# Two graph layers on one core: two batches' stages issued in turn instead of one batch after another

## The chip, the cores and the metric

The kernel runs on one core of one Trainium2 chip. The metric is the device time of one execution in microseconds; it is given as the median of several runs, and one further execution was taken with the hardware profiler. Work on the core is split over TensorE (PE; its weight loads are listed as PEld), VectorE (DVE), ScalarE (ACT), GpSimd (POOL), and the queue of SyncE (SP), which here issues transfers only. Each engine takes its instructions in the order in which the compiled program lists them.

## What is computed

There are 16 independent batches, each with 1024 nodes of 256 features (`x`, float32) and a 1024 x 1024 matrix of 0 and 1 (`adj`, int32). A batch goes through two layers.

```python
# layer 0: graph attention, 4 heads of 64
h = einsum('bnd,hde->bhne', x, W)
weight = leaky_relu(e_src[:, None] + e_dst[None, :]) where adj == 1, else -1e9   # e_* = h . a_*
out = relu(softmax(weight) @ h + bias) + h          # then a layernorm per head
x = layernorm(x + out)
# layer 1: self-attention, 8 heads of 32, queries = keys = values, then an MLP
y = layernorm(x) * gamma1 + beta1
o = x + softmax(mask(adj > 0, y y^T / sqrt(32))) @ y
o = o + (gelu(layernorm(o) @ W1 + b1) @ W2 + b2)    # 256 -> 1024 -> 256
x = layernorm(x + o)
```

The only work that crosses batches is the loading of constants. Both layers of one batch need the same mask.

## The kernel before

The program is one long list, unrolled over the 16 batches. A batch has four stages, and the next batch begins where the last stage ends.

**Preparation** (`prepare`, `masks`). The batch's `x` is loaded whole into `xb` (1 MB, by SP), turned on PE in four pieces (`transpose_rows`, L208, copied out by ACT, L209) and multiplied with the weights (`es`, L234; `h`, L243, copied out by DVE, L244). `cb` (L251, L253) holds the exponentials of the source terms for all heads and columns. `masks` takes eight row blocks of `adj`, which POOL's queue loads and casts to bf16 (L224), turns each on PE (L279), has DVE copy it from PSUM to the bf16 tile `mask` (L280), and has ACT square it for a range test (L281), after which the block's buffer is loaded again.

**Layer 0** (`attention0`, `after0`). For two column halves `n` and two head pairs, eight key blocks are gone through two at a time: four DVE instructions (L300, 128 x 512 each) make the unnormalised weights `p`, and 12 matmuls (L311, L321, column tiles of 32; float32, so each is two PE instructions) add up the products and the sums of the weights. After a half, `after0` runs for two pairs of row blocks: a chain of some 20 DVE instructions that goes over to POOL six times (L359, L373, L392 and the power function of L183) and to ACT once (L367), and that leaves `x1`, `v1` and, turned, `nT`.

**Layer 1** (`attention1`, `finish1`). There are 32 steps (two halves, two groups of four heads, eight key blocks). A step is four score matmuls (L407, row tiles of 32), ACT exponentials into two tiles `p` (L413, 128 x 1024), two DVE multiplications with the mask (L414), and, two steps later (`LAG = 2`), four product and four sum matmuls (L421, L429). `finish1` normalises a half, again over POOL (L485 to L487, L183), and its pieces are issued between later steps.

**MLP** (`mlp`). Per half, eight hidden tiles (L515, L518 with Gelu) and four output blocks (L525), each followed by a layernorm `z` on DVE and POOL (L529, L193, L188, L183, L201) and a store by SP (L531).

A tile pool has a number of buffers for each name of tile, and an instruction that writes a new tile waits until the last reader of the buffer's former tile is done. Eight PSUM banks are dealt out as `ps_s` (two tiles of two banks), `ps_t` (two of one) and `ps_o` (two of one). `mask`, `x1`, `v1`, `nT`, `xb`, and the tiles named `big` (`cb` and the MLP's hidden tile) and `fT` (`xT` and `yT`) have one buffer each, so most of the next batch can't begin before this one has let go of them. The tile `p` has seven.

The order of the program is not quite the order on the engines. What is written earlier goes first, but in the compiled list an instruction whose buffer or input was not expected to be free is passed by a later one. The trace shows it: four of the mask transposes (L279) run between the two groups of L251, which the program writes wholly before them.

Of the kernel before, what the change touches and what calls it, by code (L numbers as in the profile page):

```python
# [31 lines left out]
F32 = mybir.dt.float32  # L32
# [18 lines left out]
def fast_path(  # L51
# [47 lines left out]
    three = ctx.enter_context(tc.tile_pool(name="three", bufs=3))  # L99
    seven = ctx.enter_context(tc.tile_pool(name="seven", bufs=7))  # L100
    small = ctx.enter_context(tc.tile_pool(name="small", bufs=4))
    ps_s = ctx.enter_context(tc.tile_pool(name="ps_s", bufs=2, space=PSUM))
    ps_t = ctx.enter_context(tc.tile_pool(name="ps_t", bufs=2, space=PSUM))
# [33 lines left out]
    for src, dst in ((a_src, wsrc.rearrange("p c (h q) -> p c h q", q=Q)[:, :, :, 0]), (a_dst, w0e[:, :, D : D + H0])):  # L137
        a = one.tile([P, H0, HO, T], F32, name="big")
# [4 lines left out]
        for c in range(DC):  # L143
            t = two.tile([P, H0, HO], F32, name="nrm")
# [58 lines left out]
    def transpose_rows(dst, src, k):  # L203

        pt = ps_t.tile([P, DC, GB, P], F32, name="pt")
        for g in range(GB):
            for c in range(DC):
                nc.tensor.transpose(pt[:, c, g, :], src[:, g, c * P : (c + 1) * P], ident)  # L208
        nc.scalar.copy(dst[:, :, k * P : (k + GB) * P], pt.rearrange("p c g q -> p c (g q)"))  # L209


    xbs = {}

    def load_x(b):
        xbs[b] = one.tile([P, NB, D], F32, name="xb")
        nc.sync.dma_start(xbs[b], x[b].rearrange("(k p) d -> p k d", p=P))
# [3 lines left out]
    def load_adj(i):  # L220
        b, k = divmod(i, NB)
        if b < B:
            ak = adj_blocks[i] = three.tile([P, N], BF16, name="ak")
            nc.gpsimd.dma_start(ak, adj[b, k * P : (k + 1) * P, :])  # L224

    def prepare(xb, factors):

        xT = one.tile([P, DC, N], F32, name="fT")
        for k in range(0, NB, GB):
            transpose_rows(xT, xb[:, k : k + GB, :], k)  # L230
        es = ps_s.tile([P, NH, HALF], F32, name="ps")
        for n in range(NH):
            for c in range(DC):
                nc.tensor.matmul(  # L234
                    es[:, n, :], wsrc[:, c, :], xT[:, c, n * HALF : (n + 1) * HALF], start=c == 0, stop=c == DC - 1
                )
        esr = one.tile([P, NH, HALF], F32, name="x1")
        nc.scalar.copy(esr, es)
        h = one.tile([P, NB, D + H0], F32, name="h")
        for k in range(NB):  # L240
            ph = ps_o.tile([P, D + H0], F32, name="po")
            for c in range(DC):
                nc.tensor.matmul(ph, xT[:, c, k * P : (k + 1) * P], w0e[:, c, :], start=c == 0, stop=c == DC - 1)  # L243
            nc.vector.tensor_copy(h[:, k, :], ph)  # L244
# [769 lines left out]
```

## Time and profile before

| | |
|---|---|
| median of 3 runs | 5069.28 us (5067.32 to 5074.34) |
| profiled execution, its own time | 5062.94 us |
| span from first to last instruction | 5061.2 us |
| granted PE clock, mean over the span | 0.895 |
| busy: PE, DVE, ACT, POOL | 4257.7, 3072.4, 1632.3, 1145.1 us |
| first dense transposes of batch 0; batch 2; batch 3 | at 32.8; 656.6; 968.4 us |

The profile's page gives busy time by engine, the span in 40 slices (digits are tenths), the chain of waits followed back from the last instruction, and groups of instructions with busy time, count, mean duration and the idle time of the engine just before them, with what ended it. The trace can also be asked for stretches of time, for waits, and for single instructions in order.

### The profile page before, as it was taken

The page shows a single profiled execution, that of the slowest core. Times are in us where ns is not written, and L with a number is a line of the kernel's source. Part 1 is how long each engine was busy: PE and PEld are TensorE (multiplying, and loading weights), DVE is VectorE, ACT ScalarE, POOL GpSimd, SP SyncE. Part 2 cuts the span into 40 slices and gives each one's busy share as a digit, 9 for nine tenths or more (in the row PEclk, how much of TensorE's full clock was granted, in tenths as well). Part 3 has the DMA queues.
Part 4 walks back from the last instruction along what each step waited for, and adds up shares of the span by engine and source line. Part 5 has one row for each costly group of instructions (what it writes and reads, how often), then busy time and mean ns, then how long its engine had stood idle before and what let it go on. Part 6 is the DMA issues. An engine that isn't in the chain of part 4 may idle for free.

```text
span 5061.2 us, 60881 instructions
## 1 busy us (share of the span) xinstructions
PE 4257.7 (84%) x25121; PEld 1780.8 (35%) x25121; DVE 3072.4 (61%) x5213; ACT 1632.3 (32%) x2000; POOL 1145.1 (23%) x1160
## 2 busy tenths in 40 slices
PE   6797987979889798897978979789797897978978
PEld 3252342523325233252432524325243252422524
DVE  5647656466664656646566465664656656566565
ACT  1331424314143241432424223242232423324233
POOL 2222122221222212122121221212212122221221
PEclk9898998989889898898988989889798998988979
DMA  2000010100101001010010100101001010010000
GB/s 67 9 18 16 4 23 9 26 9 5 22 9 26 9 5 21 9 26 9 6 20 9 26 9 8 18 9 26 9 7 19 9 26 9 9 17 9 19 1 10
DMA packets 58992, 75.57 MB, mean 15 GB/s; under 512 B 7249, under 2 KB 41809, under 8 KB 58705
## 3 DMA queue, kind: packets, MB, share of 16 engines
q0 software_dynamic: 18432, 33.56, 4.3%
q1 hardware_dynamic: 35072, 33.56, 2.0%
q10 hardware_dynamic: 5200, 4.46, 0.3%
q8 instruction: 199, 3.26, 0.3%
q14 instruction: 89, 0.72, 0.0%
HBM read 88.35 MB, written 16.78 MB: 21 GB/s over the span
## 4 chain that ended last, share of the span: by engine, by line
PE 46%; DVE 24%; POOL 18%; issue 7%; ACT 2%; DMA 1%; POOLq 0%; DVEq 0%; ACTq 0%
PE ps L515 9%; PE ps L407 8%; PE po L421 7%; PE po L525 7%; PE po L429 7%; DVE p L300 6%; DVE p L414 6%; POOL r L183 5%; PE ps L311 3%; PE pt L208 2%; POOL o L373 2%; POOL v L392 2%; POOL o L485 2%; ACT p L413 2%; POOL o L359 1%
## 5 line engine op out<-in xcount | busy, mean ns | idle before, releaser
L414 DVE TENSOR_TENSOR p<-p,mask 128x1024 f32<-128x1024 f32 x1024 | 1231.5, 1235 | 403.2 <-ACT p L413 403.1
L413 ACT ACTIVATE p<-ps 128x1024 f32<-128x1024 f32 x1024 | 994.6, 1021 | 847.7 <-PE ps L407 843.9
L311 PE MATMUL ps<-p,v 128*32 128x512 f32 x4096 | 831.6, 628 | 126.3 <-DVE p L300 126.3
L407 PE MATMUL ps<-nT 32*128 32x512 f32 x4096 | 763.9, 714 | 71.2 <-ACT p L413 71.2
L300 DVE SCALAR_TENSOR_TENSOR p<-big,dinv,mask 128x512 f32<-128x512 f32 x1024 | 733.1, 757 | 1.8
L421 PE MATMUL po<-p,v 128*32 128x512 f32 x4096 | 645.8, 664 | 56.4 <-DVE p L414 56.0
L429 PE MATMUL po<-p,unit 128*32 128x512 f32 x4096 | 637.8, 642 | 0.0
L485 POOL TENSOR_TENSOR o<-o,x 128x512 f32<-128x512 f32 x64 | 110.7, 1729 | 1665.9 <-DVE o L480 1665.9
L321 PE MATMUL ps<-p,ranges 128*32 128x512 f32 x2048 | 472.8, 604 | 0.0
L407 PEld LDWEIGHTS ps<-nT 32*128 32x128 f32 x4096 | 246.2, 205 | 598.3 <-ACT p L413 443.9
L525 PE MATMUL po<-w_sb,big 128*128 128x256 f32 x2048 | 454.2, 380 | 0.0
L515 PE MATMUL ps<-fT,w_sb 128*128 128x512 f32 x1024 | 451.6, 594 | 0.0
L525 PEld LDWEIGHTS po<-w_sb,big 128*128 128x128 f32 x2048 | 385.4, 190 | 59.3 <-issue 7.7
L183 POOL TENSOR_TENSOR r<-v,mhalf 128x2 f32<-128x2 f32 (+1 forms) x320 | 218.1, 681 | 749.3 <-DVE v L188 749.3
L311 PEld LDWEIGHTS ps<-p,v 128*32 128x32 f32 x4096 | 190.7, 112 | 538.8 <-DVE p L300 359.3
L208 PE MATMUL pt<-ident,v 128*128 128x128 f32 x256 | 67.1, 413 | 299.6 <-POOL v L392 299.6
L518 ACT ACTIVATE big<-ps,b_sb 128x512 f32<-128x512 f32 x256 | 175.9, 687 | 386.1 <-PE ps L515 386.1
L515 PEld LDWEIGHTS ps<-fT,w_sb 128*128 128x128 f32 x1024 | 190.8, 190 | 228.5 <-issue 227.4
L429 PEld LDWEIGHTS po<-p,unit 128*32 128x32 f32 x4096 | 149.5, 118 | 342.1 <-issue 341.2
L529 DVE TENSOR_TENSOR z<-po,x 128x256 f32<-128x256 f32 x128 | 54.0, 422 | 354.6 <-PE po L525 354.4
L421 PEld LDWEIGHTS po<-p,v 128*32 128x32 f32 x4096 | 95.3, 112 | 444.5 <-DVE p L414 236.3
L209 ACT COPY nT<-pt 128x512 f32<-128x512 f32 x64 | 37.5, 586 | 635.6 <-PE pt L208 635.6
(105 smaller groups left out, 3726.6 us busy)
## 6 DMA issues: line engine op xcount, KB each, us to landing
ak<-in_adj_dram POOLq DMA_DIRECT2D x128, 256.0 KB, 3.7
xb<-in_x_dram SPq DMA_DIRECT2D x16, 1024.0 KB, 5.2
out_dram<-z SPq DMA_DIRECT2D x128, 128.0 KB, 1.7
w_sb<-in_L_gnn_W_dram ACTq DMA_DIRECT2D x2, 1024.0 KB, 8.3
big<-in_L_gnn_a_src_dram ACTq DMA_DIRECT2D x1, 640.0 KB, 6.3
big<-in_L_gnn_a_dst_dram ACTq DMA_DIRECT2D x1, 640.0 KB, 5.2
w0e<-in_L_gnn_W_dram ACTq DMA_DIRECT2D x8, 32.0 KB, 7.6
bias_r<-in_L_gnn_bias_dram ACTq DMA_DIRECT2D x1, 128.0 KB, 6.4
```

The costliest lines, as they stand in the source:

```text
L183: nc.gpsimd.tensor_tensor(r, src, mhalf[:, :n], op=OP.pow)
L300: nc.vector.scalar_tensor_tensor(p[:, e, :], cb[:, hd, cols], dinv[:, jb, hd : hd + 1], mask[:, jb, cols], op0=OP.max, op1=OP.mult,)
L311: nc.tensor.matmul(acc[at : at + Q, 0, :], v0[:, jb, pair * PAIR + e, q * Q : (q + 1) * Q], ps[jb][:, e, :], start=jb == 0, stop=jb == NB - 1,
L321: nc.tensor.matmul(acc[at : at + Q, 1, :], factors[:, jb, pair * PAIR + e : pair * PAIR + e + 1].to_broadcast([P, Q]), ps[jb][:, e, :], st ...
L407: nc.tensor.matmul(tiles[e // PAIR][:, e % PAIR, :], nT[q, quad, keys], nT[q, quad, cols], start=True, stop=True)
L413: nc.scalar.activation(p, t, AF.Exp, scale=SCALE1)
L414: nc.vector.tensor_mul(p, p, mask[:, jb, None, cols].to_broadcast([P, PAIR, HALF]))
L421: nc.tensor.matmul(av[e * Q : (e + 1) * Q, :], v1[:, jb, hd * HD : (hd + 1) * HD], ps[e // PAIR][:, e % PAIR, :], start=jb == 0, stop=jb = ...
L429: nc.tensor.matmul(sums[e * Q : (e + 1) * Q, :], unit[:, quad, :], ps[e // PAIR][:, e % PAIR, :], start=quad == 0 and jb == 0, stop=quad = ...
L485: nc.gpsimd.tensor_add(o, o, x1[:, blocks, :])
L515: nc.tensor.matmul(ph, w1_sb[:, c, f * P : (f + 1) * P], yT[:, c, cols], start=c == 0, stop=c == DC - 1)
L525: nc.tensor.matmul(po, hid[:, f, q * P : (q + 1) * P], w2_sb[:, f, :], start=f == 0, stop=f == FC - 1)
```

## The change

Two generators now issue the program. `layer0()` does preparation, masks and layer 0 of all batches in turn; `layer1()` does layer 1 and the MLP of all batches. Each yields a number at its cutting points, in units close to microseconds of PE work, and a loop at the end takes a piece from one or the other so that `layer0()` stays 1.15 batches ahead by these numbers. A yield of 0.0 changes neither count, so the loop goes on with the same stream there.

`mask` (now bytes), `dinv`, `x1`, `v1` and `nT` get two buffers. `x` is loaded in pieces of two row blocks (`xk`, two buffers), once for preparation and once again for `after0`; `xT` exists for two row blocks only; `cb` is made for one half and one pair at a time; `adj` blocks have two buffers instead of three; `oT` and `sT` one instead of two, and `y` is written over `o`; `p` has six buffers instead of seven, for both streams. In PSUM, `ps_s` becomes four tiles of one bank that scores, exponents, hidden tiles and all transposes share; layer 0's products and sums have two banks of their own (`ps_a`), and `ps_o` stays. A step's scores are four tiles, so ACT's exponential is four instructions of 128 x 512 instead of two of 128 x 1024.

The core of the diff:

```diff
-    three = ctx.enter_context(tc.tile_pool(name="three", bufs=3))
-    seven = ctx.enter_context(tc.tile_pool(name="seven", bufs=7))
+    six = ctx.enter_context(tc.tile_pool(name="six", bufs=6))
     small = ctx.enter_context(tc.tile_pool(name="small", bufs=4))
-    ps_s = ctx.enter_context(tc.tile_pool(name="ps_s", bufs=2, space=PSUM))
-    ps_t = ctx.enter_context(tc.tile_pool(name="ps_t", bufs=2, space=PSUM))
+    ps_s = ctx.enter_context(tc.tile_pool(name="ps_s", bufs=4, space=PSUM))
+    ps_a = ctx.enter_context(tc.tile_pool(name="ps_a", bufs=2, space=PSUM))
     ps_o = ctx.enter_context(tc.tile_pool(name="ps_o", bufs=2, space=PSUM))
...
-    def transpose_rows(dst, src, k):
-
-        pt = ps_t.tile([P, DC, GB, P], F32, name="pt")
+    def transpose_rows(dst, src):
+
+        pt = ps_s.tile([P, DC, GB, P], F32, name="ps")
         for g in range(GB):
             for c in range(DC):
                 nc.tensor.transpose(pt[:, c, g, :], src[:, g, c * P : (c + 1) * P], ident)
-        nc.scalar.copy(dst[:, :, k * P : (k + GB) * P], pt.rearrange("p c g q -> p c (g q)"))
-
-
-    xbs = {}
-
-    def load_x(b):
-        xbs[b] = one.tile([P, NB, D], F32, name="xb")
-        nc.sync.dma_start(xbs[b], x[b].rearrange("(k p) d -> p k d", p=P))
+        nc.scalar.copy(dst, pt.rearrange("p c g q -> p c (g q)"))
+
+
+    def load_x(b, k):
+        t = two.tile([P, GB, D], F32, name="xk")
+        nc.sync.dma_start(t, x[b, k * P : (k + GB) * P, :].rearrange("(g p) d -> p g d", p=P))
+        return t
...
-            ak = adj_blocks[i] = three.tile([P, N], BF16, name="ak")
+            ak = adj_blocks[i] = two.tile([P, N], BF16, name="ak")
...
+    def prepare(b, h, esr):
+
+            xk = load_x(b, k)
+            xT = two.tile([P, DC, GB * P], F32, name="xT")
+            transpose_rows(xT, xk)
+            yield 1.0
+            es = ps_s.tile([P, GB * P], F32, name="ps")
+                nc.tensor.matmul(es, wsrc[:, c, :], xT[:, c, :], start=c == 0, stop=c == DC - 1)
+            nc.scalar.copy(esr[:, k * P : (k + GB) * P], es)
+            for g in range(GB):
+                ph = ps_s.tile([P, D + H0], F32, name="ps")
+                for c in range(DC):
+                    nc.tensor.matmul(ph, xT[:, c, g * P : (g + 1) * P], w0e[:, c, :], start=c == 0, stop=c == DC - 1)
+                nc.vector.tensor_copy(h[:, k + g, :], ph)
+            yield 2.7
...
+    def masks(b, mask):
+            i = b * NB + k
+            ak = adj_blocks.pop(i)
+            pt = ps_s.tile([P, NB, P], BF16, name="ps")
+            for j in range(NB):
+                nc.tensor.transpose(pt[:, j, :], ak[:, j * P : (j + 1) * P], identb)
+            nc.vector.tensor_copy(mask[:, :, k * P : (k + 1) * P], pt)
+            nc.scalar.activation(ak, ak, AF.Square, bias=mhalf[:, 0:1], accum_out=types[:, i : i + 1])
+            load_adj(i + 2)
+            yield 1.0
...
+    def attention0(v0, esr, dinv, factors, mask, rinv, after):
...
-            oT = two.tile([P, H0 // PAIR, HALF], F32, name="oT0")
+            oT = one.tile([P, H0 // PAIR, HALF], F32, name="oT0")
             for pair in range(H0 // PAIR):
-                acc = ps_s.tile([P, 2, HALF], F32, name="ps")
+
+                cb = two.tile([P, PAIR, HALF], F32, name="cb")
+                pbs = [ps_s.tile([P, HALF], F32, name="ps") for _ in range(PAIR)]
+                for e in range(PAIR):
+                    q = slice((pair * PAIR + e) * Q, (pair * PAIR + e + 1) * Q)
+                    nc.tensor.matmul(pbs[e], spread[q, :], esr[q, cols], start=True, stop=True)
+                for e in range(PAIR):
+                    nc.scalar.activation(cb[:, e, :], pbs[e], AF.Exp, scale=0.99)
+                yield 1.0
+                av = ps_a.tile([P, HALF], F32, name="acc")
+                sums = ps_a.tile([P, HALF], F32, name="acc")
                 for j2 in range(0, NB, 2):
                     ps = {}
                     for jb in (j2, j2 + 1):
-                        p = ps[jb] = seven.tile([P, PAIR, HALF], F32, name="p")
+                        p = ps[jb] = six.tile([P, PAIR, HALF], F32, name="p")
...
+                    yield 0.0
+                    for jb in (j2, j2 + 1):
...
+                    yield 2.7
+                nc.scalar.copy(oT[:, pair, :], av)
+                sT = one.tile([P, HALF], F32, name="sT")
+                nc.vector.tensor_copy(sT, sums)
+                pt = ps_s.tile([P, BPH, P], F32, name="ps")
                 for q in range(BPH):
                     nc.tensor.transpose(pt[:, q, :], sT[:, q * P : (q + 1) * P], ident)
                 parts = pt.rearrange("p k (e i z) -> p k e i z", e=PAIR, z=Q)
-                sums = small.tile([P, BPH, PAIR], F32, name="sums")
...
+                yield from after(n * BPH + q, pt)
...
+        xl = load_x(b, k)
+        nc.gpsimd.tensor_add(xl, xl, lnb0_r[:, None, :].to_broadcast([P, GB, D]))
...
-            tiles = [ps_s.tile([P, PAIR, HALF], F32, name="ps") for _ in range(QUAD // PAIR)]
+            tiles = [ps_s.tile([P, HALF], F32, name="ps") for _ in range(QUAD)]
             for e in range(QUAD):
                 q = slice(e * HD, (e + 1) * HD)
-                nc.tensor.matmul(
-                    tiles[e // PAIR][:, e % PAIR, :], nT[q, quad, keys], nT[q, quad, cols], start=True, stop=True
-                )
+                nc.tensor.matmul(tiles[e], nT[q, quad, keys], nT[q, quad, cols], start=True, stop=True)
             ps = []
-            for t in tiles:
-                p = seven.tile([P, PAIR, HALF], F32, name="p")
-                nc.scalar.activation(p, t, AF.Exp, scale=SCALE1)
+            for e in range(0, QUAD, PAIR):
+                p = six.tile([P, PAIR, HALF], F32, name="p")
+                for i in range(PAIR):
+                    nc.scalar.activation(p[:, i, :], tiles[e + i], AF.Exp, scale=SCALE1)
                 nc.vector.tensor_mul(p, p, mask[:, jb, None, cols].to_broadcast([P, PAIR, HALF]))
...
                 ready[i] = weights(*steps[i])
-            yield
             if i < LAG:
                 continue
+            yield 1.0
             n, quad, jb = steps[i - LAG]
             if jb == 0:
                 av = ps_o.tile([P, HALF], F32, name="po")
                 if quad == 0:
                     sums = ps_o.tile([P, HALF], F32, name="po")
-                    oT = two.tile([P, H1 // QUAD + 1, HALF], F32, name="oT1")
+                    oT = one.tile([P, H1 // QUAD + 1, HALF], F32, name="oT1")
             products(n, quad, jb, ready.pop(i - LAG), av, sums)
+            yield 2.0
...
+            yield 1.75
...
+            yield 3.5
+
+
+    handed = {}
+
+    def layer0():
+        for b in range(B):
+            seen = two.tile([P, NR], F32, name="ranges")
+            rinv1 = seen[:, 0 : NB * H1].rearrange("p (k h) -> p k h", h=H1)
+            rinv0 = seen[:, NB * H1 : NB * (H1 + H0)].rearrange("p (k h) -> p k h", h=H0)
+            factors = seen[:, NB * (H1 + H0) : NR].rearrange("p (k h) -> p k h", h=H0)
+            h = one.tile([P, NB, D + H0], F32, name="h")
+            esr = one.tile([P, N], F32, name="esr")
+            yield from prepare(b, h, esr)
+            dinv = two.tile([P, NB, H0], F32, name="dinv")
+            v0 = one.tile([P, NB, H0, HO], F32, name="v0")
+            values0(h, factors, dinv, v0)
+            mask = two.tile([P, NB, N], U8, name="mask")
+            yield from masks(b, mask)
+            x1 = two.tile([P, NB, D], F32, name="x1")
+            v1 = two.tile([P, NB, D], F32, name="v1")
+            nT = two.tile([P, DC, N], F32, name="nT")
+            handed[b] = seen, rinv1, mask, x1, v1, nT
+            yield from attention0(
+                v0, esr, dinv, factors, mask, rinv0, lambda k, pt: after0(b, k, pt, rinv0, h, x1, v1, nT)
+            )
+
+    def layer1():
+        for b in range(B):
+            seen, rinv1, mask, x1, v1, nT = handed.pop(b)
+            yT = one.tile([P, DC, N], F32, name="yT")
+            late = []
+
+            def between(main):
+
+                for cost in main:
+                    yield cost
+                    if late and next(late[0], late) is late:
+                        late.pop(0)
+
+            yield from between(attention1(nT, v1, mask, lambda n, oT: late.append(finish1(n, oT, x1, rinv1, yT))))
+            yield from between(mlp(b, 0, yT, x1))
+            while late:
+                for _ in late.pop(0):
+                    yield 0.0
+            in_range(seen)
+            yield from mlp(b, 1, yT, x1)
+
+
+    WORK0 = 15.0 + 8.0 + 4 * 12.8 + 4 * 1.8
+    WORK1 = 3.0 * (NH * NB * H1 // QUAD) + NH * (1.75 * FC + 3.5 * BPH)
+    AHEAD = 1.15
+    load_adj(0)
+    load_adj(1)
+    first, second = layer0(), layer1()
+    at0, at1 = 0.0, 0.0
+    while first or second:
+        if first and (at0 <= at1 + AHEAD or not second):
+            cost = next(first, None)
+            if cost is None:
+                first = None
+            else:
+                at0 += cost / WORK0
+        else:
+            cost = next(second, None)
+            if cost is None:
+                second = None
+            else:
+                at1 += cost / WORK1
```

## The prediction, made before the changed kernel was run

> **What bounds the kernel now.** I read the busy rows and the slices first, then the chain of waits, then the time by stage of one batch, then single instructions.
>
> ```profile
> PE 4257.7 (84%) x25121; PEld 1780.8 (35%) x25121; DVE 3072.4 (61%) x5213; ACT 1632.3 (32%) x2000; POOL 1145.1 (23%) x1160
> PE   6797987979889798897978979789797897978978
> DVE  5647656466664656646566465664656656566565
> PEclk9898998989889898898988989889798998988979
> PE 46%; DVE 24%; POOL 18%; issue 7%; ACT 2%; DMA 1%; POOLq 0%; DVEq 0%; ACTq 0%
> ```
>
> No engine is full, and the chain changes hands: PE, then DVE, then POOL. The stages of batch 2 show why (preparation and masks; layer 0; steps of layer 1; MLP):
>
> ```profile
> core 0: us, PE busy (x) PEld busy (x) DVE busy (x) ACT busy (x) POOL busy (x), PEclk, DMA share, GB/s
> 655.00:699.00 44.00, 37.31 (x212) 21.69 (x214) 19.90 (x36) 18.47 (x28) 15.56 (x26) 0.81 0.33 54
> 699.00:791.00 92.00, 63.60 (x416) 21.52 (x409) 71.39 (x136) 13.07 (x18) 26.13 (x18) 0.90 0.00 1
> 791.00:911.00 120.00, 105.94 (x748) 30.15 (x747) 82.04 (x99) 58.57 (x62) 17.62 (x14) 0.92 0.03 10
> 911.00:966.80 55.80, 55.64 (x205) 36.77 (x204) 18.21 (x56) 12.05 (x18) 12.39 (x15) 1.00 0.04 15
> ```
>
> Layer 0 is DVE's (71 of 92 us), MLP is PE's (55.64 of 55.80), and the granted clock is 1.00 where PE has no gaps and down to 0.81 where it has. Two batches' stages could fill each other's gaps. A dense step of layer 1, and what POOL and DVE do to each other:
>
> ```profile
> 838.59 1.14 PE L407 MATMUL ps<-nT 32*128 32x512 f32 x8
> 839.66 1.07 PE L421 MATMUL po<-p,v 128*32 128x512 f32 x8
> 840.54 1.04 PE L429 MATMUL po<-p,unit 128*32 128x512 f32 x8
> 840.82 2.36 DVE L414 TENSOR_TENSOR p<-p,mask 128x1024 f32<-128x1024 f32 x2 [0.80 <-ACT p L413]
> 787.43 3.42 DVE L414 TENSOR_TENSOR p<-p,mask 128x1024 f32<-128x1024 f32 x2
> 787.60 2.17 POOL L392 TENSOR_TENSOR v<-v,be_r 128x512 f32<-128x512 f32 x1 [1.00 <-DVE v L389]
> ```
>
> Five L407 groups in a row start at 835.43, 838.59, 841.51, 844.66 and 847.59, so a step takes 12.16 / 4 = 3.04 us of PE, and 2.36 of DVE. Beside a POOL addition, two multiplications took 3.42 us, and the addition 2.17 against 1.26 alone: 1.06 us lost by DVE, 0.9 by POOL. DVE also waits for POOL inside the chains:
>
> ```profile
> DVE z L201 <- POOL r L183: 119.7, 128, 2.3
> DVE y L494 <- POOL r L183: 110.0, 64, 2.0
> DVE o L372 <- POOL r L183: 106.0, 64, 1.8
> DVE o L360 <- POOL o L359: 81.6, 64, 1.4
> DVE o L374 <- POOL o L373: 79.1, 64, 1.4
> ```
>
> **The present sum.** PE's dense work starts at 32.8 us and ends at about 5053, so a batch takes (5053 - 32.8) / 16 = 313.8 us; 41 us lie outside. Batch 2 splits into layer 0 with preparation, 136 us, and layer 1 with MLP, 176.
>
> **The change, part by part.** Per batch, busy times of the groups divided by 16.
>
> *DVE, layer 0 stream:* L300 733.1 / 16 = 45.8; the 20 instructions of `after0` 33.6 (seven of 0.69, the rest from their rows, four times); masks L280 5.5; L244 3.4; sums and `sT` 4.8: 93. *Layer 1 stream:* L414 77.0; `oT` copies 4.1; `finish1` 11.7; `z` 13.9; range test 1.1: 108. Little is removed.
>
> *Byte mask.* No row has a byte operand. A two-input instruction costs (1235 - 692) / 512 = 1.06 ns an element with a bf16 second input (L414) and 692 ns for 512 with a float32 one (L374, same rate), so width doesn't matter there: I take 0 for L300 and L414 (ends: 0, and 10% of 123 us). The copy L280 runs 1024 elements in 691 ns, twice that rate; at the single rate it is L414's 1235: 8 x 0.54 = 4.4 us, taken; other end 0.
>
> *Exponentials.* 64 of 1021 ns become 128 of 128 x 512; nearest rows 586 (L328) and 687 (L518); at 587, 75 us against 65, so ACT has some 115 us in a batch, table loads for the alternation of Exp and Gelu included (1.28 us each, two now, perhaps four): covered by everything. Alone, a step has 2.3 us of ACT after its scores and needs all four banks again; I add 0.3 us a step where nothing is between.
>
> *x and adj.* SP issues x in eight pieces of 256 KB, in line with the stores of `z`, so a piece may wait for a store's `z` (some 3 us of chain) and then land 3.7 us later (adj's row of the same size). Behind it PE's transposes are stuck, and in `after0` POOL's first addition and then every power of both streams. The second buffer lets a piece go out a piece earlier, and POOL sat idle before L359 for 553.9 / 64 = 8.7 us: I take 0, other end 8 x 6.7 = 54 us. Two adj buffers instead of three: PE waited 82.7 us in all for adj now; blocks come at wider spacing, 0 taken, ends -5 and +10 a batch.
>
> *`ps_a`.* A pair's next product waits for ACT's copy (0.59) and DVE's `sT` (0.68): 4 x 1.5 = 6 us of the layer 0 stream, covered by the other stream; uncovered 6.
>
> **Where the overlap ends.** By the counts in the code, layer 1's 32 steps are 96 of 152 units, so they run beside the layer 0 stream from 0.15 to 0.78 of its order: masks, three of the four pairs, two `after0`. There:
> - PE: 32 x 3.04 = 97; 12 groups of 24 matmuls at 2.58 us (708.92 to 711.50) = 31; mask transposes 7; others 7; exponents 4.6: 147 us.
> - DVE: steps, `oT`, half of `finish1` 87; masks at the new price 9.9, L300 34.4, sums 3.6, two `after0` 16.8: 152. To that, waits for POOL in order, which hold back what is queued behind them on DVE, weights of both streams: 358.6 / 64 = 5.6 an `after0` (rows L372, L360, L374, L389, L381) and 2.8 a `finish1`: 17. And collisions with POOL: some 18 additions of this stretch at 1.06 are 19; 8 of it is in the means already (757 against the least L300, 693, 48 times; 1235 against the least L414, 1156, 64 times): 11. In all 180 us.
>
> So DVE sets this stretch. MLP's stretch is PE's: 55.8, one pair 10.3, prepare 13.4, transposes and exponents 5.5: 85, DVE 55. With 5 us for what I count at nothing above, a batch takes 180 + 85 + 5 = 270 us.
>
> The SBUF page of the Trainium skill (Who interferes with whom) speaks against the change: a VectorE instruction with two SBUF inputs and a GpSimd one that reads SBUF block each other wholly. The row L414 beside L392 agrees. If each of POOL's 24 wide additions in a batch cost DVE 1.06 us, a batch would be 25 - 11 = 14 us longer.
>
> The TensorEngine Tiling page (Key Properties) says that a change of tile shape drains TensorE, and this change alternates shapes more often. In the step above the scores, the one change of shape and back, take 1.07 against 0.88 for the products. If some 60 more changes came at 0.2 us, a batch would be 12 us longer.
>
> Layer 0 runs alone for 1.15 batches at the start, layer 1 with MLP for 1.15 at the end: 41 + 1.15 x 136 + 1.15 x 176 + 1.15 x 32 x 0.3 = 41 + 156 + 202 + 11 = 410 us. Between lie 14.85 batches: 14.85 x 270 = 4010. Span 4420; the profiled execution's own time is 1.7 more than its span (5062.94 against 5061.2), and the median of the runs 6.3 more than that: 4428 us.
>
> **The rivals.** *A, PE bounds.* The compiled order fills DVE's waits with the other stream's work, and PE's 147 + 85 + 5 = 237 us remain: 410 + 14.85 x 237 + 8 = 3937. For it: windows of layer 0 with DVE at 8.00 of 8. Against: the waits for POOL above exist although other work was ready.
>
> *B, shared buffers.* At the cut after a step's scores three steps hold all six `p`; layer 0 gets none until products are done. A score group needs all four `ps_s` banks, and a bank with a transpose is let go only when DVE, the fullest engine, has read it. Some 44 such uses a batch, at 0.7 us of stall each, add 30: 300 us, 410 + 14.85 x 300 + 8 = 4873.
>
> *C, slower: lockstep.* In a single `p` and `ps_s` ring both streams release each other's buffers in turn, PE waits in order for a layer 0 group whose L300 sit behind L414 whose exponentials wait for PE, and the batches add up as now: 313.8, plus 32 x 0.3 for the exponentials, 4.4 for the mask, 6 for `ps_a`: 334 us, 41 + 16 x 334 + 8 = 5393. It decides once the overlap hides less than 20 us of a batch. Against it: the stretches of 8 us from 832 to 856 have PE and DVE both above 5.5 of 8, over `p` buffers that are one more than the new ones.
>
> That the streams don't mix is a rival only in part: the yields of 0.0 cut nothing, so four L300 and their matmuls always come together; it belongs to B.
>
> **The numbers.** Forecast (255 to 290 a batch, 4200 to 4720 us) 0.44; A (231 to 255, 3850 to 4200) 0.17; B (290 to 312, 4720 to 5050) 0.19; C 0.18; no change 0.02. The range of 3850 to 5050 leaves out C and no change, 2 in 10. The dearest unknowns of the byte mask, x and adj are held by B's part of it. Faster 0.80, same 0.02, slower 0.18; 0.2% is about what a measurement of this kernel can tell from no change.
>
> **What the profile after would show.** Right: slices without the period of a batch in them but for the two ends; DVE at 75% or more and PE at about 90% of the middle; clock near 1.0; L280 at 1.2 us; a distance of 270 us between batches; waits of DVE for POOL as long as now. A shows PE without gaps in layer 1's stretch. B and C show PE's L407 waiting for ACT or DVE reading `ps`, and L300 for L311's release of `p`. Wrong would be a step of layer 1 that grows beyond 5.6 us (180 / 32) on average, L300 or L414 longer with bytes, or waits for `xk`.

## The result and the profile after

The changed kernel takes 6025.65 us (median of 4 runs, 6015.99 to 6029.76) against 5069.06 of the kernel before in the same comparison: ratio 1.1882 [1.1862, 1.1903], 957 us slower. The forecast was 4428, with a range up to 5050. Line numbers below are those of each run's own program, one or two off from each other: the turning of `nT` is L208 before, L207 after.

The page of the changed kernel, busy row, slices, clock and chain:

```profile
PE 4653.2 (77%) x25249; PEld 1940.2 (32%) x25249; DVE 3197.8 (53%) x5213; ACT 1730.3 (29%) x3146; POOL 1130.8 (19%) x1096
...
PE   4777877779777787777877778777787777879778
...
DVE  4554654646545465554654546545465454655544
...
PEclk7788988889888898888988888888898888989889
...
PE 52%; DVE 21%; POOL 13%; issue 7%; ACT 4%; DMA 1%; POOLq 0%; ACTq 0%; DVEq 0%
```

The slices are flatter than before, but flat at 7 and 8: PE fell from 84% to 77%, DVE from 61% to 53%, where the forecast wanted 75%, and the mean granted clock from 0.895 to 0.86. The first transposes of `xk` of the third batch start at 582.12 us, those of the fourteenth at 4702.96: (4702.96 - 582.12) / 11 = 374.6 us a batch, where 270 were forecast and 313.8 stood before. Cut up, about one batch (start of layer 1; its steps; the same with the second half's chains; MLP; MLP's end with the next chains) is:

```profile
core 0: us, PE busy (x) PEld busy (x) DVE busy (x) ACT busy (x) POOL busy (x), PEclk, DMA share, GB/s
2124.30:2150.00 25.70, 21.52 (x121) 7.60 (x118) 18.39 (x14) 15.67 (x31) 12.13 (x11) 0.87 0.16 27
2150.00:2290.00 140.00, 117.28 (x746) 35.39 (x746) 86.64 (x116) 49.39 (x95) 16.67 (x16) 0.93 0.07 11
2290.00:2380.00 90.00, 66.60 (x340) 23.78 (x344) 48.91 (x76) 24.06 (x43) 12.79 (x11) 0.76 0.02 6
2380.00:2420.00 40.00, 36.79 (x196) 20.93 (x188) 20.80 (x51) 5.88 (x9) 13.26 (x12) 1.00 0.03 10
2420.00:2496.70 76.70, 46.56 (x180) 32.81 (x180) 24.45 (x71) 12.81 (x21) 17.79 (x18) 0.78 0.10 29
```

The stretch of the steps was to be filled by DVE and has it 62% busy; MLP's last stretch, once PE's without a gap, has PE 61% busy. From the first score of a batch to its last pass 239 us on the mean of the third to the thirteenth batch, where 180 were forecast for layer 1's stretch, and 135 from there to the next batch's first score, where the forecast had 85 + 5 = 90. Waits name two causes (engine, tile, line, what it waited for: us in total, times, longest):

```profile
DVE p L413 <- ACT p L412: 1014.8, 435, 7.4
...
PE ps L207 <- POOL v L390: 932.0, 64, 17.8
ACT p L412 <- PE acc L314: 889.5, 157, 11.5
```

The first two were, before:

```profile
DVE p L414 <- ACT p L413: 403.1, 291, 7.5
PE pt L208 <- POOL v L392: 299.6, 64, 8.1
```

**The first cause, a chain with PE idle.** PE in order of time beside one end of layer 0 (start, duration, idle time before it):

```profile
2044.10 0.60 PE L338 MATMUL ps<-ident,oT 128*128 128x128 f32 x4
2044.53 3.62 PE L521 MATMUL po<-w_sb,hid 128*128 128x256 f32 x16
2062.17 1.12 PE L207 MATMUL ps<-ident,v 128*128 128x128 f32 x4 [14.02 <-POOL v L390]
2063.08 1.06 PE L338 MATMUL ps<-ident,oT 128*128 128x128 f32 x4
2080.73 1.11 PE L207 MATMUL ps<-ident,v 128*128 128x128 f32 x4 [16.59 <-POOL v L390]
2081.64 2.76 PE L514 MATMUL ps<-yT,w_sb 128*128 128x512 f32 x3
```

Each `after0` leaves PE idle for most of a chain. The next hidden tiles (L514) of the other batch don't depend on it, and stand behind it. What follows a gap is slower as well: four L338 took 0.60 us at 2044.10 and take 1.06 at 2063.08. **The second, a step cut in two.** PE and then DVE in the densest shared part:

```profile
2181.25 1.12 PE L407 MATMUL ps<-nT 32*128 32x512 f32 x2
2182.95 1.20 PE L304 MATMUL acc<-p,v 128*32 128x512 f32 x6 [0.59 <-DVE p L291]
...
2186.69 1.13 PE L407 MATMUL ps<-nT 32*128 32x512 f32 x6
2187.76 1.07 PE L420 MATMUL po<-p,v 128*32 128x512 f32 x8
2188.64 1.04 PE L428 MATMUL po<-p,unit 128*32 128x512 f32 x8
2189.61 1.12 PE L407 MATMUL ps<-nT 32*128 32x512 f32 x2
2191.65 1.20 PE L304 MATMUL acc<-p,v 128*32 128x512 f32 x6 [0.92 <-DVE p L291]
```

```profile
2182.07 2.73 DVE L291 SCALAR_TENSOR_TENSOR p<-cb,dinv,mask 128x512 f32<-128x512 f32 x4
2188.48 2.36 DVE L413 TENSOR_TENSOR p<-p,mask 128x1024 f32<-128x1024 f32 x2 [3.68 <-ACT p L412]
2190.76 2.73 DVE L291 SCALAR_TENSOR_TENSOR p<-cb,dinv,mask 128x512 f32<-128x512 f32 x4
```

The first score of a step goes out, then a whole group of layer 0, then the other three. ACT and DVE have one quarter of a step to work on meanwhile, and DVE idles 3.68 us. A step with a group takes 2191.65 - 2182.95 = 8.70 us, where the forecast's two parts make 3.04 + 2.58 = 5.62. On the mean of all 32 steps it is 239 / 32 = 7.5, where the forecast had 5.6. In PE's records a group stands between the scores of one step 178 times.

### The profile page after: what moved, and what is told of

Same layout as the page of the kernel before. It is cut to its first block, busy times and chain, and to the rows that moved or that the text cites. A ratio compares the mean times of both kernels' runs of the same rounds, so it can differ in the third digit from the quotient of the medians.

```text
span 6027.2 us, 62833 instructions
## 1 busy us (share of the span) xinstructions
PE 4653.2 (77%) x25249; PEld 1940.2 (32%) x25249; DVE 3197.8 (53%) x5213; ACT 1730.3 (29%) x3146; POOL 1130.8 (19%) x1096
## 4 chain that ended last, share of the span: by engine, by line
PE 52%; DVE 21%; POOL 13%; issue 7%; ACT 4%; DMA 1%; POOLq 0%; ACTq 0%; DVEq 0%
PE acc L304 10%; PE ps L407 10%; PE ps L514 6%; PE po L521 6%; DVE p L413 6%; PE acc L314 5%; PE po L420 4%; POOL r L182 4%; PE po L428 4%; DVE p L291 3%; ACT p L412 3%; PE ps L207 2%; POOL v L260 2%; POOL o L356 2%; POOL o L485 1%
## 5 line engine op out<-in xcount | busy, mean ns | idle before, releaser
L412 ACT ACTIVATE p<-ps 128x512 f32<-128x512 f32 x2048 | 1074.3, 602 | 1319.7 <-PE acc L314 889.5
L407 PE MATMUL ps<-nT 32*128 32x512 f32 x4096 | 1101.7, 700 | 54.3 <-DVE mask L250 34.9
L304 PE MATMUL acc<-p,v 128*32 128x512 f32 x4096 | 815.0, 693 | 168.2 <-DVE p L291 166.7
L207 PE MATMUL ps<-ident,v 128*128 128x128 f32 x256 | 71.3, 434 | 932.0 <-POOL v L390 932.0
L291 DVE SCALAR_TENSOR_TENSOR p<-cb,dinv,mask 128x512 f32<-128x512 f32 x1024 | 737.8, 778 | 45.5 <-ACT cb L281 23.3
L314 PE MATMUL acc<-p,ranges 128*32 128x512 f32 x2048 | 622.4, 640 | 0.0
L514 PE MATMUL ps<-yT,w_sb 128*128 128x512 f32 x1024 | 508.8, 633 | 0.0
L521 PE MATMUL po<-w_sb,hid 128*128 128x256 f32 x2048 | 463.2, 380 | 1.2 <-ACT hid L515 1.2
L521 PEld LDWEIGHTS po<-w_sb,hid 128*128 128x128 f32 x2048 | 383.9, 190 | 77.3 <-issue 23.5
L304 PEld LDWEIGHTS acc<-p,v 128*32 128x32 f32 x4096 | 192.2, 117 | 657.9 <-DVE p L291 368.8
L207 PEld LDWEIGHTS ps<-ident,v 128*128 128x128 f32 x256 | 45.7, 217 | 976.2 <-POOL v L390 976.2
L208 ACT COPY nT<-ps 128x512 f32<-128x512 f32 x64 | 37.5, 586 | 854.3 <-PE ps L207 854.3
L514 PEld LDWEIGHTS ps<-yT,w_sb 128*128 128x128 f32 x1024 | 195.4, 204 | 195.7 <-issue 194.2
```

Source lines behind the costliest of these rows:

```text
L291: nc.vector.scalar_tensor_tensor(p[:, e, :], cb[:, e, :], dinv[:, jb, hd : hd + 1], mask[:, jb, cols], op0=OP.max, op1=OP.mult,)
L304: nc.tensor.matmul(av[at : at + Q, :], v0[:, jb, pair * PAIR + e, q * Q : (q + 1) * Q], ps[jb][:, e, :], start=jb == 0, stop=jb == NB - 1,)
L314: nc.tensor.matmul(sums[at : at + Q, :], factors[:, jb, pair * PAIR + e : pair * PAIR + e + 1].to_broadcast([P, Q]), ps[jb][:, e, :], star ...
L407: nc.tensor.matmul(tiles[e], nT[q, quad, keys], nT[q, quad, cols], start=True, stop=True)
L412: nc.scalar.activation(p[:, i, :], tiles[e + i], AF.Exp, scale=SCALE1)
L514: nc.tensor.matmul(ph, w1_sb[:, c, f * P : (f + 1) * P], yT[:, c, cols], start=c == 0, stop=c == DC - 1)
```

## The experiments

**Theory.** Take, for each PSUM tile, the first PE instruction that writes it. In the compiled lists of both kernels these stand, among tiles of one name (`ps`, `pt`, `po`, `acc`), in the program's order without one exception, while neighbours of different names have changed places 218 times before and 180 after. So nothing that needs a `ps` tile passes the turning of `nT` that waits for `after0`. Scores, exponents, `es` and hidden tiles had the name `ps` already; the change put all transposes and `h` under it too. (A name is a ring of buffers as well as an order; the runs don't tell these two apart.) **Rivals:** the small buffers (`p`, `adj`, bytes, single banks) set the time; or the weave itself does harm.

### Without the weave, and the small edits alone

`e1_serial`: the changed kernel with a batch's two halves issued one after the other.

```diff
-        if first and (at0 <= at1 + AHEAD or not second):
+        if first and (at0 < int(at1 + 0.005) + 0.995 or not second):
```

> All other edits kept, only the weave undone: a batch's layer 0 stream is issued whole, then its layer 1 stream. Theory 1 (the weave itself is what costs: the chains of after0 and the L0 groups stand in PE's order in front of the other stream's work): the time falls back to the old one plus the price of the supporting edits, 313.8 + 10 (exponentials in four) + 4 (mask) + 6 (one pair of accumulators) a batch: 5200 to 5450 us, and PE's wait for POOL before the nT transposes falls from 932 to about 300 us. Rival (the supporting edits cost: single banks, six p, x in pieces, bytes): 5800 to 6100 us.

Measured: 6065.52 us, ratio 1.1949 [1.192, 1.1979]: the rival's time. The weave hides 40 us in all; the loss lies in what was changed to make room for it. PE's wait for adj is 304.3 us (82.7 before), and at the turning of `nT` it is not the 300 that I expected (busy us, mean ns | idle time before, and what ended it):

```profile
L207 PE MATMUL ps<-ident,v 128*128 128x128 f32 x256 | 71.3, 434 | 1100.8 <-POOL v L390 1100.8
```

The steps of layer 1 that follow each other with nothing between them (four or more in a row) take 3.18 us on the mean against 3.07 before, so four exponentials cost about 0.1 us a step, not 0.3.

`e3_lag1`: `LAG = 1`, so that layer 1 holds four of the six `p`.

```diff
-        LAG = 2
+        LAG = 1
```

> Only LAG = 2 becomes 1, so that layer 1 holds four p instead of six and layer 0's group finds two free. Rival 1b (groups wait for p): L413's wait for ACT falls from 1015 to about 600 us and the time to 5500 to 5700 us. Theory 1a: no gain beyond 100 us, and perhaps a loss where layer 1 runs alone, 5950 to 6200 us.

Measured: 6096.51 us, ratio 1.201 [1.198, 1.2041]: two free `p` alone are not it. The run says more about the second cause. The four scores go together again (a group stands between them 21 times, not 178), and nothing is gained: DVE's wait for the exponentials is 1093.7 us, and a step with a group, from 2217.64 to 2226.83, takes 9.19 us, because PE's L304 waits for L291. So the cut alone is not the cost: a group that stands in PE's order before its `p` are written costs as much uncut.

`e4_bytes`: the kernel before with a byte mask and nothing else.

```diff
-        mask = one.tile([P, NB, N], BF16, name="mask")
+        mask = one.tile([P, NB, N], U8, name="mask")
```

> The kernel before with nothing but the mask tile as bytes. As the prediction has it: the mask's copy goes from 0.69 to 1.23 us (128 times, 69 us of DVE), the two-input instructions stay at 757 and 1235 ns; where the copies lie in the masks stage, DVE waits for PE 220 us in all, so the time rises by 0 to 70 us: 5069 to 5140. If bytes slowed the two-input reads, it would be above 5200.

Measured: 5132.12 us, ratio 1.0107 [1.0087, 1.0128]. Groups of DVE in that run:

```profile
L414 DVE TENSOR_TENSOR p<-p,mask 128x1024 f32<-128x1024 f32 x1024 | 1231.5, 1236 | 417.6 <-ACT p L413 417.6
L300 DVE SCALAR_TENSOR_TENSOR p<-big,dinv,mask 128x512 f32<-128x512 f32 x1024 | 729.8, 761 | 0.0
L280 DVE CAST mask<-pt 128x1024 uint8<-128x1024 bf16 x128 | 154.7, 1223 | 219.6 <-PE pt L279 219.2
```

The readers keep their pace (1235 and 757 ns before), the copy goes from 691 to 1223 ns: 54 us (0.0107 x 5075), 3.4 a batch.

`e10_before_ak2`: the kernel before with two adj buffers.

```diff
-            ak = adj_blocks[i] = three.tile([P, N], BF16, name="ak")
+            ak = adj_blocks[i] = two.tile([P, N], BF16, name="ak")
...
-            load_adj(i + 3)
+            load_adj(i + 2)
```

> The kernel before with two buffers for adj blocks instead of three (a block's successor but one is requested after its square). Accounting of the run without the weave: PE's wait for adj grows from 82.7 to some 300 us, time 5069 + 200 = 5270, ratio 1.04. Prediction's term: between -5 and +10 us a batch, 0 taken: 4990 to 5230, 5069 taken. If the wait in that run came from masks that could not pass other ps tiles instead, the ratio is within 1.01.

Measured: 5128.39 us, ratio 1.0111 [1.0078, 1.0144]; PE's wait for adj 118.4 us. The 200 us that I expected from the wait in `e1_serial` were too many; two buffers cost 56 us, 3.5 a batch.

### The shared name

`e9_before_shared`: the kernel before, its transposes taken from the scores' pool.

```diff
-    ps_s = ctx.enter_context(tc.tile_pool(name="ps_s", bufs=2, space=PSUM))
-    ps_t = ctx.enter_context(tc.tile_pool(name="ps_t", bufs=2, space=PSUM))
+    ps_s = ctx.enter_context(tc.tile_pool(name="ps_s", bufs=3, space=PSUM))
...
-        pt = ps_t.tile([P, DC, GB, P], F32, name="pt")
+        pt = ps_s.tile([P, DC, GB, P], F32, name="ps")
```

(and so for the other five kinds)

> The kernel before with one edit: its six kinds of transposes are taken from the scores' pool and name (ps_s, now three tiles of two banks), and ps_t is gone; nothing is woven, no other buffer changes. Theory 2 (tiles of one name are taken in program order, so nothing that needs a ps tile passes the turning of nT, which waits for after0): the wait of the transposes for POOL's addition, 64 times 4.7 us now (299.6), grows towards the 17.2 us of the run without the weave (1100.8 / 64), since the next half's layer 0 groups, which need a ps tile, can no longer go ahead of it; time 5069 + some 600 to 800 = 5650 to 5870, ratio 1.11 to 1.16. Rival (the shared name costs little; what costs is the small buffers and the single banks): within 100 us of before, ratio below 1.02.

Measured: 5394.16 us, ratio 1.0635 [1.0604, 1.0666]. PE's waits:

```profile
PE ps L207 <- POOL v L391: 1096.1, 64, 18.7
```

With no weave and no buffer fewer, the name takes the wait from 299.6 to 1096.1, close to the 1100.8 of `e1_serial`. The mechanism is shown. The time rose by 322 us only (0.0635 x 5075), so my 600 to 800 was too much: the wait grew by 796, but PE's busy time fell from 4257.7 to 3883.8, most of it in layer 0's products (L311 before, L310 here: 831.6 to 531.9 us). The edit also gives the scores and these products a third tile of two banks, so the 322 us are the name's price less what that tile earned; the two are not separated.

`e11_streams`: the changed kernel, layer 0's PSUM tiles under a name of their own in the two banks of `ps_a`.

```diff
-            pbs = [ps_s.tile([P, HALF], F32, name="ps") for _ in range(PAIR)]
+            pbs = [ps_a.tile([P, HALF], F32, name="acc") for _ in range(PAIR)]
```

(and so for its transposes, `es`, `h` and masks; scores, hidden tiles and `finish1` keep `ps`)

> The changed kernel with one edit: all PSUM tiles of the layer 0 stream (transposes, exponents, h, products and sums) take the name acc in the two banks of ps_a, and only layer 1 and the MLP use the four banks of ps_s. Theory 2: the turning of nT no longer stands before any score, so PE's wait for after0's POOL step falls from 932 to under 400 us and the time from 6026 to 5300 to 5600 (ratio 1.05 to 1.10), less than the wait's fall because layer 0 alone, at the start, has two banks. Rival (p and the lockstep set the time): still within 150 us of 6026, with DVE's wait for the exponentials as large as now (1014.8).

Measured: 5518.18 us, ratio 1.0879 [1.0848, 1.0911]: 508 us gained by names alone, over the same eight banks, though the wait stays above the 400 us that I expected. PE's waits:

```profile
PE acc L207 <- POOL v L390: 474.7, 64, 17.8
PE acc L304 <- DVE p L291: 186.1, 158, 3.2
```

`e5_serial_pools`, `e6_pools`: another split, transposes in one bank `ps_t`, scores and the rest in three of `ps_s`, without and with the weave.

```diff
-    ps_s = ctx.enter_context(tc.tile_pool(name="ps_s", bufs=4, space=PSUM))
+    ps_s = ctx.enter_context(tc.tile_pool(name="ps_s", bufs=3, space=PSUM))
+    ps_t = ctx.enter_context(tc.tile_pool(name="ps_t", bufs=1, space=PSUM))
```

> The kernel of e1 (no weave) with the six kinds of transposes taken out of ps_s into a pool of their own with one bank, ps_s keeping three. Theory 2 (in the compiled lists the tiles of one name are taken in program order, so what shares ps_s with the nT transposes can't pass them while they wait for after0's chain): the wait of PE's L207 for POOL falls from 1101 us to under 400, and the time from 6066 to 5250 to 5500 us. Rival 2b (the second oT, the two-bank accumulators or x in pieces hold back the next half): 5900 us or more.

> The changed kernel, weave and all, with the same separate pool for transposes. Theory 2: layer 1's steps and MLP can pass the waiting transposes, L207's wait for POOL falls from 932 to under 200 us and the time from 6026 to 5000 to 5300 us. Rival 1a (the order in which the pieces are issued is what counts, buffers aside): above 5800 us.

Measured: 6130.11 us, ratio 1.2065 [1.203, 1.21], and 5944.18, 1.1699 [1.1665, 1.1733]. Both are in the rivals' ranges. Without the weave PE's wait for `after0` falls to 329.8 us, near before's, yet the time doesn't: a step's four scores have three banks, and a step takes 4.8 us. That is 1.6 us more, 512 times, some 830 us: the misplaced bank costs what the name gives. With the weave the wait falls to 560.2 us only, for the turning of `nT` still shares its name, now `pt`, with all other transposes.

### Cuts inside the chain, and p

A yield of 0.0 lets nothing in, so the program's order itself holds a chain together. `e2_cuts`: both cuts of `after0` get a cost.

```diff
-        yield 0.0
+        yield 6.0
```

> The two yields of 0.0 inside after0 become yields of 6.0 (and WORK0 grows by as much), so that some 7 us of layer 1's work is issued between the three parts of the chain. Theory 1a (PE stands before the nT transposes because nothing of the other stream is issued inside the chain): PE's wait for POOL L390 falls from 932 to under 350 us, the time to 5400 to 5600 us. Rival 1b (the loss sits in layer 0's groups, which wait for p and split the scores): under 150 us gained, 5880 to 6000 us.

Measured: 5660.73 us, ratio 1.1152 [1.1123, 1.1181], 365 us faster than the changed kernel but not the 5600 that I expected at most. PE's wait for `after0` falls from 932.0 to 200.4 us, since scores now stand before the turning; its wait for `finish1`, under the same name, grows from 108.5 to 263.8.

`e7_pools_cuts` is `e6_pools` with these cuts; `e8_pools_cuts_p` has also `LAG = 1` and `p` split in two for layer 0 and four for layer 1.

```diff
-                        p = ps[jb] = six.tile([P, PAIR, HALF], F32, name="p")
+                        p = ps[jb] = pair0.tile([P, PAIR, HALF], F32, name="p0")
```

> e6 with the cuts of e2 in after0 as well. If pool order and cuts cure the same wait, the time is within 100 us of e6; if they add, 200 us or more under it, at 4800 to 5050 us.

> e7 with LAG = 1 and p dealt out by stream: two buffers for layer 0, four for layer 1. Theory 3 (p in one ring makes the streams take turns): L413's wait for ACT falls by 300 us or more against e7, and the time by 150 to 400 us. Rival (LAG = 1 leaves too little between a step's scores and its products, as e3 hints with 6097 against 6026): the time rises by 50 to 150 us.

Measured: 5746.04 us, ratio 1.1309 [1.1277, 1.1342], and 5480.94, 1.0788 [1.0752, 1.0823]. The cuts gain 198 us over `e6_pools`, but with cuts the one bank of `ps_t` is worse than the shared four (`e2_cuts`). Own `p` for each stream, six as before, gain 265 us, as expected: DVE's wait for the exponentials falls from 949.0 to 368.5 us, and a group stands between the scores of a step 12 times instead of 217. The run changes `LAG` too, but `LAG = 1` alone gained nothing (`e3_lag1`), and with `LAG = 2` `e14_later_p26` below has 22 such cuts; so I put the gain down to the split, and the second cause is the ring of `p` that the streams share.

`e12_streams_cuts_p8`: names of `e11_streams`, cuts of `e2_cuts`, `p` split four and four (`LAG = 1`), eight instead of six; `cb`, `sq` and `xT` get one buffer to make room.

```diff
-                cb = two.tile([P, PAIR, HALF], F32, name="cb")
+                cb = one.tile([P, PAIR, HALF], F32, name="cb")
```

> As the run before it, and the two cuts in after0 are real (yield 6.0, counted in WORK0), p is split into four tiles for layer 0 and four for layer 1 (LAG = 1), room for them from single buffers for cb, sq and xT. If the streams then share no ring of tiles, the prediction's sum should come into reach: 270 to 300 us a batch, 4430 to 4900 us, ratio 0.87 to 0.97. If the order of the list itself holds the streams together (layer 0's groups between the first and the other scores of a step), it stays above before: 5100 to 5400.

Measured: 4987.82 us, ratio 0.9834 [0.9805, 0.9862]: faster than the kernel before, and between the two times expected. The same place as above, PE in order of time:

```profile
2116.76 1.14 PE L408 MATMUL ps<-nT 32*128 32x512 f32 x8
2117.83 1.92 PE L305 MATMUL acc<-p,v 128*32 128x512 f32 x16
2119.57 1.04 PE L315 MATMUL acc<-p,ranges 128*32 128x512 f32 x8
2120.43 1.04 PE L421 MATMUL po<-p,v 128*32 128x512 f32 x8
2121.29 1.04 PE L429 MATMUL po<-p,unit 128*32 128x512 f32 x8
2122.26 1.14 PE L408 MATMUL ps<-nT 32*128 32x512 f32 x8
```

All four scores go together again, PE has no gap, and a step with a group takes 5.50 us; the group itself takes 2.60 (2117.83 to 2120.43), where it took 3.74 in the cut step (2182.95 to 2186.69). How the gain divides among the three edits is not separated.

### The waits that were left

`e13_later` adds to this two more steps before `finish1` turns its rows; `e14_later_p26` and `e15_later_p35` split `p` two and six or three and five (`LAG = 2`); `e16_later_group` is `e13_later` with a real cut ahead of layer 0's matmuls.

```diff
             yield
             yield
+            yield
+            yield
             transpose_rows(yT[:, :, k * P : (k + GB) * P], o, ps_s, "ps")
...
-                    yield 0.0
+                    yield 1.3
                     for jb in (j2, j2 + 1):
...
-                    yield 2.7
+                    yield 1.4
```

(the first two lines: all four runs; the yields of 1.3 and 1.4: the last)

> The version with own PSUM names, real cuts and p split 4 and 4, with one edit: finish1 waits two steps longer before it turns its rows (four yields instead of two). If PE's waits add up to the time, the wait for DVE o (225.9 us, 64 times) falls under 60 and the time by some 150 us, to 4840 (ratio 0.955). If the pace of PE's own work holds the time, the wait moves elsewhere and the time stays within 40 us of 4988.

> As the later finish1, and p split two (layer 0) and six (layer 1, LAG = 2) instead of four and four (LAG = 1). PE's wait of the products for L414 (129 us) goes, the wait of layer 0's groups for L292 (42 us) grows, since DVE can't write the next pair of p while a group reads one: I expect it to lose more than it wins, 20 to 100 us slower than the four and four.

> As the later finish1, and p split three (layer 0) and five (layer 1, LAG = 2). Between the two others: the wait of the products for L414 falls from 129 to under 60 us, layer 0's wait for L292 grows from 42 to some 100; within 60 us of the four and four.

> As the later finish1, and a real cut between layer 0's four L292 and the group's 12 matmuls (yields of 1.3 and 1.4 in place of 0.0 and 2.7), so that a piece of layer 1 may be issued between them. Expected: L305's wait for L292 (42 us) falls, DVE's L414 waits less for exponentials; 0 to 100 us faster than the later finish1 alone.

Measured, in this order: 4853.57 us, ratio 0.9563 [0.9522, 0.9604]; 4840.15, 0.9537 [0.9483, 0.959]; 4917.35, 0.9689 [0.9647, 0.973]; 4821.29, **0.9499 [0.946, 0.9539]**, the fastest. In `e13_later` the wait for `finish1` fell from 225.9 to 61.1 us and the time by 134: PE's waits do add up now. I had expected two and six to lose 20 to 100 us, and they didn't: the intervals of the two overlap. Three and five lost 64 us, with a busier PE (4338.4 against 4206.1 us); no run shows why.

`e17_all` joins two and six, the cut and cuts of 8.0; `e18_all_serial` is the same kernel without the weave (the edit of `e1_serial`).

> The repairs together: own PSUM names for the two streams, finish1 two steps later, a cut of 1.3 before layer 0's matmuls, p split two and six with LAG = 2, and the cuts in after0 of 8.0, about a chain's 17 us in two. From the single runs (4821 with the cut before the matmuls; 4840 against 4854 for two and six; PE's wait for after0 137 us, of which four waits of up to 17.8 at the start can't go): 4750 to 4830 us, ratio 0.936 to 0.952.

> The same kernel with the weave undone: layer0 and layer1 of a batch issued one after the other, everything else equal. If the weave is what earns the gain, this is slower than before by what the small buffers and the two banks of layer 0 cost: 5500 to 6000 us. If the other repairs earn it, it lies within 150 us of the woven one.

Measured: 4831.71 us, ratio 0.9513 [0.9483, 0.9542], no better than `e16_later_group`; and 6050.17, ratio 1.1918 [1.1875, 1.1961], above what I expected. So the weave is worth 6050 - 4832 = 1218 us with own names and the other repairs, and 6066 - 6026 = 40 in the changed kernel. Most of the 1218 only wins back what the new buffers lose without it; against the kernel before, the gain is 5%. PE's wait at `nT` in the two, unwoven and woven:

```profile
PE acc L208 <- POOL v L391: 804.0, 64, 17.8
```

```profile
PE acc L208 <- POOL v L391: 133.6, 31, 17.8
```

The page of `e16_later_group`:

```profile
PE 4174.6 (87%) x25249; PEld 1760.0 (37%) x25249; DVE 3164.2 (66%) x5213; ACT 1705.9 (35%) x3136; POOL 1131.3 (23%) x1096
...
PE   5588888889888899889898888898889988888898
...
PEclk8789999999999999999999999999899999999999
```

From the first transposes of its third batch to those of its fifteenth (505.44 to 4018.07 us) it takes 292.7 us a batch.

## Why the prediction was wrong

**The step that failed** is "where the overlap ends": it fills one stream's waits with the other's work, and its sum for PE has no term for PE's own wait at the turning of `nT`, which was 299.6 / 16 = 18.7 us a batch before. I had read the order as one in which an instruction that waits is passed by a later one, and the example for it, mask transposes between two groups of L251, was of two names, `pt` and `ps`. Within a name nothing passes (not one first use), and the change merged the names. `e9_before_shared` shows it without a weave, `e11_streams` without any other repair. Rival B had the shared banks at 44 uses of 0.7 us; what they cost is not the release of a bank but a wait for a chain, 14.6 us on the mean and up to 17.8, 64 times, with both streams behind it: 932.0 / 16 = 58 us a batch. That is over half of the 105 us between forecast and result; the ring of `p` that both streams share, which rivals B and C did name, is a further part (265 us between `e7_pools_cuts` and `e8_pools_cuts_p`, 17 a batch). That the yields of 0.0 cut nothing I named and left in B; with cuts at these places the time falls by 365 us (`e2_cuts`).

**The second error, the base.** Rival C, lockstep at 334 us a batch, came nearest: the batches do add up, and it named the rings `p` and `ps_s`, though not the chain. But I built its sum on the present 313.8 plus small prices, so that its 5393 us are still 633 short. Without the weave the new buffers take 6066 us, about 376 a batch, because in the kernel before other names could pass a chain: there PE's wait at `nT` was 299.6 us, and 1100.8 in `e1_serial`. Of those 990 us (6065.52 - 5075.39) the shared name is 322, two adj buffers 56, bytes 54, each from its own run on the kernel before. If these add up, 560 or so stay open; since the 322 are less what a third score tile earned, the name's own part may be larger. Rows of `e1_serial` point at `cb` made per half (DVE's first instruction waits 140.2 us for it, layer 0's DVE row waited 1.8 before) and at `finish1` (158.1 us of PE's wait against 78.5); neither was run alone.

**DVE as the bound** of layer 1's stretch at 180 us didn't show. The shared step took 8.70 us with PE, ACT and DVE waiting in turn, and where `p` is split PE is nearest to its bound: in `e16_later_group`, from 1000 to 4000 us, PE is busy 2649.94 us (88%) and DVE 2014.09 (67%). PE's share of a batch there is 0.88 x 292.7 = 258 us, against the 237 of rival A, which named the right engine, with 35 us of gaps that it left out. DVE's waits for POOL were as long as forecast: the five rows summed to 496 us before and to 460 in the changed kernel (112.6, 93.4, 92.0, 86.7 and 75.6), so POOL's chain didn't get slower either.

**What held.** The ends: 6027.2 - 14.85 x 374.6 = 464 us outside the middle, against 410 (472 in `e16_later_group`). The byte copy: 0.53 us more each, as taken from L414's rate, and 3.4 us a batch for 4.4. Adj: 3.5 a batch in the kernel before, within the ends of -5 and +10, though I took 0. The exponentials: about 0.1 us a step for 0.3, too much by 0.2 x 32 x 1.15 = 7 us.

**The two rules that were weighed.** In the dense part of `e12_streams_cuts_p8` a step with a group takes 5.50 us, less than 3.04 + 2.58 for the two apart. The group stands beside the products there, which are column tiles too, so the step has two changes of shape, as many as a step alone: the 60 more changes behind the 12 us a batch did not arise in it. The page TensorEngine Tiling (Array Packing), Key Properties, of the Trainium skill states that drain; no run here shows its price. In `e16_later_group` L292 has a mean of 747 ns and L414 of 1250, against 757 and 1235, and all of DVE's busy time grew by 92 us over the kernel before, of which the byte copy is 67 (88.5 to 155.3), so the 14 us a batch for POOL's additions did not come either. The SBUF page (Who interferes with whom) has the two engines block each other; the pair shown in the prediction, 3.42 against 2.36 us, agrees, but over a whole kernel these means hardly move.

## What to carry to other kernels

Before two streams are woven, list the rings of buffers in program order and ask what stands behind an instruction that waits for a long chain: a name shared by both streams makes them one queue, whatever the engines could do. Give each stream names of its own, in PSUM and for a tile like `p`, before giving it more buffers, and put real work into the list at the places where a chain crosses to another engine. Reckon the rival in which the streams don't mix from what the new buffers cost without the weave, not from the old kernel's time.

## What the runs showed of the hardware that was not expected

The step of layer 1 alone, on the mean of steps that follow each other with nothing between them, took 3.07 us with two double score tiles, 3.18 with four single ones (`e1_serial`), and 2.95 with three double ones (`e9_before_shared`), so a third tile was worth about what the smaller exponentials cost. The granted clock fell where PE had gaps (PE's busy time is the fourth number, the clock the third from the end):

```profile
2062.00:2081.00 19.00, 2.23 (x9) 1.84 (x10) 7.98 (x20) 1.22 (x2) 6.93 (x7) 0.50 0.05 14
2150.00:2200.00 50.00, 46.97 (x310) 14.47 (x314) 32.24 (x34) 22.89 (x46) 2.63 (x5) 1.00 0.19 30
```

In the first stretch PE was busy for 2.23 of 19 us, in the second for 46.97 of 50.
